# Second attention of a hybrid block: weight sums pinned in program order, the second group's weights loaded ahead of v's copies, the first group's squares in the probabilities' buffers

## The chip, the core and the metric

The kernel runs on one core of one Trainium2 chip, everything in 32-bit floats. The metric is the device time of one launch in microseconds (us); the kernel before was run three times, with a median of 1585.06 us (1583.94 to 1586.10). One more execution was profiled. Its own time was 1586.24 us, of which the profile covers a span of 1584.5 us.

The engines are TensorE (PE, matmuls, with its weight load PEld beside it), VectorE (DVE), ScalarE (ACT), GpSimd (POOL) and SyncE (SP, which issues most DMAs). Each works through its own list of instructions in order and waits where an operand isn't there yet.

## The reference, cut to what matters

The block takes x of 1024 tokens by 512 channels and applies four residual stages: a causal attention with 32 heads of 16 channels, a feed-forward layer with low-rank experts, a second attention, and the feed-forward layer again. The change lies in the second attention:

```python
q = (x @ Wq.T).reshape(b, s, 32, 128).transpose(0, 2, 1, 3)
k = (x @ Wk.T).reshape(b, s, 8, 128).transpose(0, 2, 1, 3)      # v likewise
q, k = _rmsnorm(q, q_norm_w), _rmsnorm(k, k_norm_w)
scores = einsum('bkgqd,bksd->bkgqs', q by groups of 4, k) / sqrt(128)
bias = where(rel > 0, NEG_INF, slope * rel)                      # ALiBi, causal
attn = softmax(scores + bias)
out = einsum('bkgqs,bksd->bkgqd', attn, v);  x = x + out @ Wo.T
```

Here x is layer-normalised before it goes in. There are 8 groups; each has one head of k and v and 4 heads of q.

## The kernel before, in words

**Stages.** The first attention and its feed-forward layer run to about 449 us of the trace, the second attention from there to about 1505 us, the last feed-forward layer to the end. The second attention works group by group (g = 0 to 7), head by head (hh = 0 to 3), and in a head by row tiles of 128 queries (i), from 7 down to 0. A tile's name carries these numbers: p0_1_4 is the scores and then probabilities of group 0, head 1, row tile 4.

**One row tile** (`softmax`, L1044). PE makes the scores of as many keys as the causal mask leaves, in parts of at most 512 keys (L1053). DVE multiplies each part by the query's norm and adds the bias (L1055), takes the row's maximum (L1059) and scales it (L1060); ACT makes the exponentials and their sum (L1062), DVE the reciprocal (L1064), POOL scales the row (L1065). Two row tiles later (`LAG = 2`) `finish` hands it to `columns`, where DVE transposes it in blocks into the tiles pT and tT (L1080, L1086), which leaves p's buffer free. p has four buffers. After a head's last tile PE makes the product with v (`product`, L1114: 128 or more matmuls, 5.6 us), and after the fourth head what is left of all four (`product_rest`).

**Projections by seven products.** Keys and values of a group (`project_kv`, L905), and the queries of two heads at a time (`project_q`, L969; r = 0 or 1), are made by a scheme like Strassen's (`seven`, L865): weights and tokens are each cut into 2 by 2 blocks, and seven products of sums of blocks replace eight products of blocks. Product m takes `left[m]` of the weights and `right[m]` of the tokens, and accumulates in one of two PSUM banks; order `EARLY` is 1, 2, 6, 7, 5, 4, 3 and `STEADY` 1, 6, 2, 7, 5, 4, 3.

- The tokens' sums are made once, a row of 128 columns at a time, by `token_forms` (L848): r5 and r6 on DVE (L851, L852), r7 on POOL (L853), r4 on DVE (L854). Two of the four calls come before the first products, two after the first ones.
- The weights' sums are made in place for each projection by `weight_forms` (L856), both on POOL: a21 += a22 (L861) and then s2 = a21 - a11 into a tile of its own (L862; s_kv or s_q below). Products 5 and 6 read these. Two more sums follow inside `seven`, on POOL too: `left[7]` (L878) after product 1 and `left[3]` (L881) after product 2.
- Keys and queries are normalised late: ACT squares the keys, POOL takes a power for rk (`rsqrt`, L121) and scales the keys (L940), PE transposes them. For queries, ACT squares a head's queries into one work tile that has a single buffer (`square`, L1006; the list `squares` holds heads that wait for it), PE sums the squares with a matmul by ones into a tile of pool `ps_m`, DVE transposes the sums, and POOL takes the power that gives rq (`sum_ready`, `sum_squares`).

**v's copies.** `copies` (L896) spreads each half of v over partitions into va with 16 DMAs on SyncE's queue (L903). The products read va.

**Loads.** `load_qkv` (L796) issues on the same queue the group's wkv (one DMA for k, one for v, L799) and wq (one DMA). wkv and wq have one buffer each, so a group's weights can land only when the projections of the group before are done with them. It is called for group g + 1 at the head of group g.

**How it is interleaved.** Within group g, the work for group g + 1 is cut into small units that a generator `fill` gives out: the keys' and values' projection, `boundary` (one call of `sum_ready`), the out-projection of group g - 1 (`project_o`, L760, not in group 0; it ends in a DMA by POOL that adds into xd, L773), and the two query projections. After each row tile's scores, `fill` is advanced to a number `due`: the group's units (42 in group 0, 74 in the others) times the share of the row tiles done (`SHARE`), capped by `before`, which holds the last 14 units back until after the 26th row tile. In group 0 a second cap of 14 units holds until the 10th.

Entry to the second attention: group 0's weights are loaded early. The code calls `token_forms` for two columns, makes the generators `kv` and `q`, and advances them in turn for 14 units, so that the keys' and the first queries' projections run side by side; then the second query projection follows, and two calls of `sum_ready`.

**What sets the order on an engine.** An instruction that is marked by `tc.keep_in_program_order` is placed where the program's text puts it. All others are placed by a list scheduler, which at build time picks for each engine among the instructions whose operands it models as ready, the earliest in the program first, and those under `tc.high_priority` ahead of them. Before the change the weights' sums are not marked, and the scheduler puts them into gaps of POOL's list.

Of the kernel before, what the change touches and what calls it, by code (L numbers as in the profile page):

```python
# [9 lines left out]
F32 = mybir.dt.float32  # L10
# [54 lines left out]
class Block:  # L65
# [677 lines left out]
    def attention_b(self, ctx, wo_pool, WqT, WkT, WvT, WoT, qw, kw, xnT, xd, missing, ffn_weights):  # L743
# [44 lines left out]
        with ExitStack() as ctx:  # L788
# [4 lines left out]
            ps_m = ctx.enter_context(tc.tile_pool(name="b_m", bufs=2, space=PSUM))  # L793
            ps_o = ctx.enter_context(tc.tile_pool(name="b_o", bufs=1, space=PSUM))

            def load_qkv(g, pinned=False):  # L796
                wkv = wp.tile([P, KC, 2, DB], F32, tag="wkv", name=f"wkv{g}")
                for n, src in enumerate((WkT, WvT)):
                    dma = nc.sync.dma_start(  # L799
                        wkv[:, :, n, :], src[:, g * DB : (g + 1) * DB].rearrange("(k p) n -> p k n", p=P)  # L800
                    )
                    if pinned:
                        tc.keep_in_program_order(dma)
                wq = wp.tile([P, KC, GRP * DB], F32, tag="wq", name=f"wq{g}")
# [3 lines left out]
                return wq, wkv  # L808
# [7 lines left out]
            wq, wkv = load_qkv(0, pinned=True)  # L816


            rels = [self.rel, cp.tile([P, T], F32, tag="relr", name="relr")]
# [28 lines left out]
            def token_forms(a):  # L848

                r = {m: t[:, :, a * P : (a + 1) * P] for m, t in right.items()}  # L850
                nc.vector.tensor_sub(r[5], r[5], r[1])  # L851
                nc.vector.tensor_sub(r[6], r[3], r[5])  # L852
                nc.gpsimd.tensor_tensor(r[7], r[6], r[1], ALU.subtract)  # L853
                nc.vector.tensor_sub(r[4], r[2], r[6])  # L854

            def weight_forms(w, name):  # L856

                blocks = [[w[:, h * H : (h + 1) * H, n] for h in range(2)] for n in range(2)]
                (a11, a12), (a21, a22) = blocks
                s2 = work.tile([P, H, DB], F32, tag="s2", name=f"s2_{name}")  # L860
                nc.gpsimd.tensor_tensor(a21, a21, a22, ALU.add)  # L861
                nc.gpsimd.tensor_tensor(s2, a21, a11, ALU.subtract)  # L862
                return {1: a11, 2: a12, 3: a12, 4: a22, 5: a21, 6: s2, 7: a11}

# [37 lines left out]
                    for a in range(P // B):  # L902
                        nc.sync.dma_start(to[a * B : (a + 1) * B, :, b, :], v_sb[b * B : (b + 1) * B])  # L903

            def project_kv(g, wkv):  # L905
                vs[g] = []
                kT = kTs[g] = kvp.tile([P, T], F32, tag="kT", name=f"kT{g}")
                halves = [kT[:, h * QC : (h + 1) * QC].rearrange("p (i d) -> p i d", d=DB) for h in range(2)]
# [14 lines left out]
                            yield  # L923

                def done():
                    copies(g, 0, v_sb[0])
                    if g:
                        kept.append((g, 1, v_sb[1]))
                    else:
                        copies(g, 1, v_sb[1])  # L930
                    for half, k_sb in enumerate(halves):
                        ssq = sm.tile([P, 4], F32, tag="ssq", name=f"ssq{g}_{half}")
                        for a in range(4):
                            sq = work.tile([P, DB], F32, tag="ksq", name=f"ksq{g}_{half}_{a}")
# [10 lines left out]
                yield from seven(  # L945
                    lambda m: ps_m.tile([P, 4, DB], F32, tag="m", name=f"kv{g}_{m}"),
                    multiply,
                    weight_forms(wkv, f"kv{g}"),
                    *halves,
                    *v_sb,  # L950
                    order=STEADY if g else EARLY,
# [17 lines left out]
            def project_q(g, wq, r, pool=ps_m, tag="m"):  # L969

                if not r:
                    qTs[g] = []
# [16 lines left out]
                            yield  # L989

                def done():
                    squares.extend((g, 2 * r + n) for n in range(2))
                    square()

                if later and (g or r):
# [1 line left out]
                yield from seven(  # L997
                    lambda m: pool.tile([P, QC], F32, tag=tag, name=f"pq{g}_{r}_{m}"),
                    multiply,
                    weight_forms(wq.rearrange("p k (n d) -> p k n d", d=DB)[:, :, 2 * r : 2 * r + 2], f"q{g}_{r}"),  # L1000
                    *(t[:, h * QC : (h + 1) * QC] for t in pair for h in range(2)),
                    order=STEADY if g or r else EARLY,
                    done=done,
# [10 lines left out]
            def sum_ready(behind=False):  # L1014
# [2 lines left out]
                    sum_squares(*squared.pop(0), behind)  # L1017
                square()

            def sum_squares(g, hh, sq_T, behind):  # L1020

                rq = rqs[g][hh]
                st = ps_m.tile([P, QC], F32, tag="m", name=f"st{g}_{hh}")[:, : NT * B]
                for a, sq in enumerate(sq_T.rearrange("p (i a c) -> a p i c", a=P // B, c=B)):
                    with ExitStack() as ctx:
                        if behind:
# [143 lines left out]

            LAG = 2
            wo = load_o(0)
            for a in range(2):
                token_forms(a)
            kv, q = project_kv(0, wkv), project_q(0, wq, 0, ps_s, "s")
            for n in range(7 * H):
                next(kv)  # L1180
                next(q)
# [3 lines left out]
            for n, _ in enumerate(in_turn(kv, q, project_q(0, wq, 1))):  # L1185
                if n == 3:
                    k_columns(*later.pop(0))
            for _ in range(2):
                sum_ready()
            pending = []  # L1190
            fill = iter(())
            heads = list(range(GRP))
# [32 lines left out]
            for g in range(HKV):  # L1225
# [14 lines left out]
                units = 42 + 32 * (g > 0)  # L1240
# [1 line left out]
                for hh in range(GRP):  # L1242
# [205 lines left out]
```

## Time and profile before

| | us |
|---|---|
| median of three runs | 1585.06 |
| the profiled execution's own time | 1586.24 |
| its span | 1584.5 |
| busy: PE | 1548.3 |
| busy: DVE / ACT / POOL | 1079.5 / 594.7 / 486.3 |
| PE busy from 0 to 373 us (first attention) | 369.0 of 373 |
| 373 to 449 (first feed-forward layer) | 76.0 of 76 |
| 449 to 600 (entry and group 0 of the second attention) | 130.0 of 151 |
| 600 to 1505 (its other groups) | 900.8 of 905 |
| 1505 to 1584.5 (last feed-forward layer) | 72.5 of 79.5 |

The first columns of a profile line give a start and a busy time, then the engine, the source line, the operation, the tile written and the tiles read, with sizes in partitions by elements; what stands in brackets is how long the engine had been idle just before, and what it was waiting for. Idle time of an engine costs only where the end of the program depends on it. The granted clock is the share of TensorE's full rate that the chip allowed; over the whole span it was 0.993, and from 449 to 600 us 0.93.

### The profile page before, as it was taken

Reading aid. Unit: us, or ns where it says so; the run is one execution under the profiler, and the core shown is the slowest. Engines: PE = TensorE matmul, PEld = TensorE weight load, DVE = VectorE, ACT = ScalarE, POOL = GpSimd, SP = SyncE. Lnnn points to the kernel's source line nnn. Section 1 sums busy time; section 2 is a strip of 40 time slices with the busy share of each in tenths; the row PEclk is TensorE's granted clock in tenths of the full one; section 3 lists DMA queues with packets and bytes.
Section 4 is the critical chain, followed back from the end, with each engine's and each line's share of the span. In section 5 each row is a group of like instructions: output and inputs, shape, how many; then the busy total and the mean of one; then the engine's idle time right before and its main releaser. Section 6 shows DMA issues by size and latency. Waiting matters only on the chain.

```text
span 1584.5 us, 32254 instructions
## 1 busy us (share of the span) xinstructions
PE 1548.3 (98%) x12894; PEld 928.6 (59%) x12894; DVE 1079.5 (68%) x2789; ACT 594.7 (38%) x1277; POOL 486.3 (31%) x639
## 2 busy tenths in 40 slices
PE   9999999999988899999999999999999999999999
PEld 5545555555555556656755755755665675556664
DVE  4557778773545786777678667677777866777753
ACT  2216656664212433333333333243333333333330
POOL 3000000002243524433443433343344343333450
PEclk9999999999999989999999999999999999999999
DMA  5000222220123101330330231242133022135001
GB/s 206 1 1 6 20 22 19 17 20 18 45 82 94 41 1 53 62 60 28 81 52 21 69 61 41 54 72 50 42 66 67 28 61 35 40 74 126 10 2 53
DMA packets 80951, 75.34 MB, mean 48 GB/s; under 512 B 14945, under 2 KB 56673, under 8 KB 80801
## 3 DMA queue, kind: packets, MB, share of 16 engines
q1 hardware_dynamic: 70272, 52.56, 14.2%
q0 software_dynamic: 8848, 17.58, 7.7%
q10 hardware_dynamic: 1680, 3.15, 0.5%
q8 instruction: 101, 1.65, 0.4%
q14 instruction: 50, 0.40, 0.1%
HBM read 33.08 MB, written 18.87 MB: 33 GB/s over the span
## 4 chain that ended last, share of the span: by engine, by line
PE 86%; DVE 6%; POOL 4%; issue 1%; SPq 1%; ACT 1%; DMA 1%; DVEq 0%; POOLq 0%; ACTq 0%
PE s L1053 14%; PE pq L980 11%; PE o L1114 11%; PE wo L765 11%; PE sT L407 8%; PE kv L914 5%; PE oT L449 5%; PE or L1114 4%; PE pm_f L714 3%; PE s L358 3%; PE pj_v L218 2%; PE pj_q L218 2%; PE pm_ao L1322 2%; PE pj_k L218 2%; DVE p L1055 1%
## 5 line engine op out<-in xcount | busy, mean ns | idle before, releaser
L1062 ACT ACTIVATE p<-p,nm 128x1024 f32<-128x1024 f32 (+7 forms) x256 | 198.4, 775 | 415.5 <-DVE nm L1060 383.3
L1065 POOL TENSOR_SCALAR p<-p,rs 128x1024 f32<-128x1024 f32 (+7 forms) x256 | 192.0, 750 | 406.3 <-DVE rs L1064 392.4
L1053 PE MATMUL s<-kT,qT 128*128 128x512 f32 (+3 forms) x768 | 300.5, 503 | 16.2 <-DVE p L1055 10.9
L1053 PEld LDWEIGHTS s<-kT,qT 128*128 128x128 f32 x768 | 139.4, 192 | 184.2 <-issue 111.4
L765 PE MATMUL wo<-wo,oT 128*128 128x512 f32 x512 | 237.9, 593 | 0.9 <-ACT spare L781 0.9
L1080 DVE STREAM_TRANSPOSE pT<-p 128x512 f32<-128x512 f32 (+3 forms) x256 | 153.9, 603 | 106.5 <-POOL p L1065 63.7
L1059 DVE TENSOR_REDUCE nm<-p 128x1 f32<-128x1024 f32 (+7 forms) x256 | 188.0, 735 | 2.6
L429 ACT ACTIVATE p<-sT 128x512 f32<-128x512 f32 (+1 forms) x292 | 155.2, 592 | 91.0 <-PE s L358 35.2
L1114 PEld LDWEIGHTS o<-pT,va 32*128 32x128 f32 x4212 | 172.9, 185 | 22.3 <-issue 12.5
L1114 PE MATMUL o<-pT,va 32*128 32x224 f32 (+5 forms) x4212 | 181.3, 324 | 0.5 <-DVE pT L1080 0.5
L358 PE MATMUL s<-kT,qT 32*128 32x512 f32 (+3 forms) x768 | 165.2, 520 | 0.0
L407 PE MATMUL sT<-qT,kT 32*128 32x128 f32 (+3 forms) x1152 | 155.9, 402 | 0.7 <-DMA qT<-negT 0.7
L765 PEld LDWEIGHTS wo<-wo,oT 128*128 128x128 f32 x512 | 94.2, 190 | 90.3 <-issue 78.1
L1055 DVE SCALAR_TENSOR_TENSOR p<-s,rq,relr 128x512 f32<-128x512 f32 x192 | 121.4, 648 | 13.6 <-PE s L1053 11.3
L980 PE MATMUL pq<-xnTb,wq 128*128 128x512 f32 x256 | 123.7, 593 | 0.1
L1055 DVE SCALAR_TENSOR_TENSOR p<-s,rq,rel 128x512 f32<-128x512 f32 (+1 forms) x192 | 103.0, 559 | 16.5 <-PE s L1053 16.4
L407 PEld LDWEIGHTS sT<-qT,kT 32*128 32x128 f32 x1152 | 80.8, 184 | 51.0 <-issue 29.4
L1086 DVE STREAM_TRANSPOSE tT<-p 128x512 f32<-128x512 f32 (+3 forms) x128 | 63.9, 499 | 58.1 <-POOL p L1065 30.5
L375 DVE TENSOR_REDUCE part<-s 128x1 f32<-128x512 f32 x128 | 81.6, 685 | 28.1 <-PE s L358 20.1
L508 POOL TENSOR_TENSOR o<-o,over 64x512 f32<-64x512 f32 x12 | 15.2, 1270 | 270.9 <-DMA o<-oTs 113.6
L1064 DVE RECIPROCAL rs<-ss 128x1 f32<-128x1 f32 x256 | 39.9, 156 | 73.6 <-ACT p L1062 73.1
L449 PE MATMUL oT<-p,v_p 128*32 128x128 f32 (+1 forms) x1552 | 88.8, 331 | 0.8 <-DVE turned L472 0.8
(188 smaller groups left out, 2103.9 us busy)
## 6 DMA issues: line engine op xcount, KB each, us to landing
va<-v SPq DMA_DIRECT2D x256, 64.0 KB
xd<-beside POOLq DMA_DIRECT2D x56, 256.0 KB, 4.1
wq<-in_b_WqT_dram SPq DMA_DIRECT2D x8, 1024.0 KB
wo<-in_b_WoT_dram SPq DMA_DIRECT2D x8, 1024.0 KB
x_x<-in_x_dram SPq DMA_DIRECT2D x8, 256.0 KB
wkv<-in_b_WkT_dram SPq DMA_DIRECT2D x8, 256.0 KB
xd<-x_x ACTq DMA_DIRECT2D x8, 256.0 KB
wkv<-in_b_WvT_dram SPq DMA_DIRECT2D x8, 256.0 KB
```

Of the source, the lines that this page charges most:

```text
L358: nc.tensor.matmul(made[j][:, at:end], lhsT=qT[rows_of(j), c, i * P : (i + 1) * P], rhs=kT[rows_of(j), c, kc * QC : kc * QC + end - at], s ...
L407: nc.tensor.matmul(made[j][:, at:end], lhsT=kT[rows_of(j), c, b * P : (b + 1) * P], rhs=qT[rows_of(j), c, qc * QC + x0 : qc * QC + x1], st ...
L429: nc.scalar.activation(p[:, j, :end], made[j][:, :end], AF.Exp)
L449: nc.tensor.matmul(o[rows_of(j), x0 + p0 - at : x0 + p1 - at], lhsT=v_cols(b, c * HC + j), rhs=p[:, j, p0:p1], start=first, stop=last,)
L765: nc.tensor.matmul(ps, lhsT=oTs[g, h][:, t * P : (t + 1) * P], rhs=wo[:, h, :], start=(h == heads[0]), stop=(h == heads[-1]))
L980: nc.tensor.matmul(ps, lhsT=w[:, kc, :], rhs=x[:, kc, :], start=first and kc == 0, stop=kc == H - 1, skip_group_check=True,)
L1053: nc.tensor.matmul(s, lhsT=qT[:, i * P : (i + 1) * P], rhs=kT[:, lo:hi], start=True, stop=True)
L1055: nc.vector.scalar_tensor_tensor(p[:, lo:hi], s, rq[:, i : i + 1], rels[i % 2][:, at + lo : at + hi], ALU.mult, ALU.add)
L1059: nc.vector.tensor_reduce(nm, p[:, :w], AX.X, ALU.max, negate=True)
L1062: nc.scalar.activation(p[:, :w], p[:, :w], AF.Exp, bias=nm, scale=slope, accum_out=ss)
L1065: nc.gpsimd.tensor_scalar(p[:, :w], p[:, :w], rs, 1.0, ALU.mult, ALU.mult)
L1114: nc.tensor.matmul(cols(o[:, a], j, j + skip), lhsT=vs[g][j // 4][rows, j % 4 * NB + b, :], rhs=moving(j, j + skip, rows, slice(b * B, (b ...
```

## The change

All of it lies in the second attention.

- `weight_forms` marks its first sum (a21 += a22) to stay in program order, except for the keys and values and both query projections of group 0. The second sum is not marked. POOL therefore meets the marked sum at the place where the generator that makes it is first advanced (for keys and values, at the head of the group before), behind everything that the program's text puts ahead of it on POOL and that is marked or ready.
- `load_qkv` is split. Group 1's wkv is loaded in `project_kv`'s `done` for group 0, so its two DMAs are issued before v's copies of group 0. The other groups' loads stay where they were.
- At the entry, the weights' sums for the keys and values and for the first queries of group 0 come before the tokens' sums in the program's text; r7 of `token_forms` moves from POOL to DVE.
- Group 0's squares go into four buffers of p's pool as soon as a query projection is done, and the sums of squares into the tile of `ps_o`, the products' PSUM pool. The sums are asked for after units 6 and 9 of the second query projection, and the rest right after the first row tile's scores. The other groups keep the single work tile.
- Group 0's `due` loses both caps, and the order of its fill becomes: keys and values of group 1, first queries, `boundary`, second queries.

```diff
-            def load_qkv(g, pinned=False):
+            def load_kv(g, pinned=False):
...
+            def load_q(g, pinned=False):
...
-                nc.gpsimd.tensor_tensor(r[7], r[6], r[1], ALU.subtract)
+                nc.vector.tensor_sub(r[7], r[6], r[1])
...
-            def weight_forms(w, name):
+            def weight_forms(w, name, pinned=True):
...
-                nc.gpsimd.tensor_tensor(a21, a21, a22, ALU.add)
+                first = nc.gpsimd.tensor_tensor(a21, a21, a22, ALU.add)
+                if pinned:
+                    tc.keep_in_program_order(first)
                 nc.gpsimd.tensor_tensor(s2, a21, a11, ALU.subtract)
...
                 def done():
+                    if not g:
+                        loaded.append(load_kv(1))
                     copies(g, 0, v_sb[0])
...
-                    weight_forms(wkv, f"kv{g}"),
+                    forms,
...
+            def q_forms(g, wq, r):
+                return weight_forms(wq.rearrange("p k (n d) -> p k n d", d=DB)[:, :, 2 * r : 2 * r + 2], f"q{g}_{r}", g > 0)
...
                 def done():
+                    if not g:
+                        for hh in (2 * r + 1, 2 * r):
+                            sq = pp.tile([P, T], F32, tag="p", name=f"qsq{g}_{hh}")
+                            nc.scalar.activation(sq, qTs[g][hh], AF.Square)
+                            squared.append((g, hh, sq))
+                        return
                     squares.extend((g, 2 * r + n) for n in range(2))
                     square()
...
-                st = ps_m.tile([P, QC], F32, tag="m", name=f"st{g}_{hh}")[:, : NT * B]
+                if g:
+                    st = ps_m.tile([P, QC], F32, tag="m", name=f"st{g}_{hh}")[:, : NT * B]
+                else:
+                    st = ps_o.tile([P, NB, QC], F32, tag="o", name=f"st{g}_{hh}")[:, 0, : NT * B]
...
+            kv = project_kv(0, weight_forms(wkv, "kv0", False))
+            q = project_q(0, wq, 0, ps_s, "s", q_forms(0, wq, 0))
             for a in range(2):
                 token_forms(a)
-            kv, q = project_kv(0, wkv), project_q(0, wq, 0, ps_s, "s")
...
-            for _ in range(2):
-                sum_ready()
+                if n in (6, 9):
+                    sum_ready()
+            wkv = loaded[0]
...
-                    wq, wkv = load_qkv(g + 1)
-                    parts.append(project_kv(g + 1, wkv))
-                parts.append(boundary())
+                    if g:
+                        wkv = load_kv(g + 1)
+                    wq = load_q(g + 1)
+                    forms = weight_forms(wkv, f"kv{g + 1}")
+                    parts.append(project_kv(g + 1, forms))
                 if g:
-                    parts.append(project_o(g - 1, wo, heads, ps_m, "m"))
-                if not last:
-                    parts.extend(project_q(g + 1, wq, r) for r in range(2))
+                    parts.extend((boundary(), project_o(g - 1, wo, heads, ps_m, "m")))
+                    parts.extend(() if last else (project_q(g + 1, wq, r) for r in range(2)))
+                else:
+                    parts.extend((project_q(1, wq, 0), boundary(), project_q(1, wq, 1)))
...
+                        while not g and squared and squared[0][0] == 0:
+                            sum_ready()
...
-                            before = 7 * H if not g and n <= NT + LAG else units - 7 * H if n <= 3 * NT + LAG else units
-                            due = min(due, before)
-                            if n in (3 * NT + LAG, 0 if g else NT + LAG):
-                                due = before
+                            if g and n <= 3 * NT + LAG:
+                                due = min(due, units - 7 * H)
+                                if n == 3 * NT + LAG:
+                                    due = units - 7 * H
```

More of the change, by code (lines that the diff above doesn't have):

```diff
@@ L803, in load_qkv @@
                         tc.keep_in_program_order(dma)
+                return wkv
+            def load_q(g, pinned=False):
                 wq = wp.tile([P, KC, GRP * DB], F32, tag="wq", name=f"wq{g}")
@@ L807, in load_qkv @@
                     tc.keep_in_program_order(dma)
-                return wq, wkv
+                return wq
             def load_o(g):
@@ L813, in load_o @@
                 return wo
-            wq, wkv = load_qkv(0, pinned=True)
+            wkv, wq = load_kv(0, pinned=True), load_q(0, pinned=True)
             rels = [self.rel, cp.tile([P, T], F32, tag="relr", name="relr")]
@@ L903, in copies, with project_kv @@
                         nc.sync.dma_start(to[a * B : (a + 1) * B, :, b, :], v_sb[b * B : (b + 1) * B])
-            def project_kv(g, wkv):
+            def project_kv(g, forms):
                 vs[g] = []
@@ L967, in k_columns, with project_q @@
                 nc.scalar.activation(k_sb, ps, AF.Copy, scale=kqw)
-            def project_q(g, wq, r, pool=ps_m, tag="m"):
+            def q_forms(g, wq, r):
+                return weight_forms(wq.rearrange("p k (n d) -> p k n d", d=DB)[:, :, 2 * r : 2 * r + 2], f"q{g}_{r}", g > 0)
+            def project_q(g, wq, r, pool=ps_m, tag="m", forms=None):
                 if not r:
@@ L999, in project_q @@
                     multiply,
-                    weight_forms(wq.rearrange("p k (n d) -> p k n d", d=DB)[:, :, 2 * r : 2 * r + 2], f"q{g}_{r}"),
+                    forms or q_forms(g, wq, r),
                     *(t[:, h * QC : (h + 1) * QC] for t in pair for h in range(2)),
@@ L1018, in sum_ready @@
                 square()
+            loaded = []
             def sum_squares(g, hh, sq_T, behind):
                 rq = rqs[g][hh]
-                st = ps_m.tile([P, QC], F32, tag="m", name=f"st{g}_{hh}")[:, : NT * B]
+                if g:
+                    st = ps_m.tile([P, QC], F32, tag="m", name=f"st{g}_{hh}")[:, : NT * B]
+                else:
+                    st = ps_o.tile([P, NB, QC], F32, tag="o", name=f"st{g}_{hh}")[:, 0, : NT * B]
                 for a, sq in enumerate(sq_T.rearrange("p (i a c) -> a p i c", a=P // B, c=B)):
```

## The prediction

> **What bounds the kernel now.** I read the page's busy times first, then TensorE (PE) in stretches of time, then the timelines of PE, GpSimd (POOL) and SyncE's queue (SPq) inside the poor stretches. The rows by stretch give the busy time of PE, its weight load, DVE, ACT and POOL, then the granted clock, the DMA share and GB/s. In the timelines the columns are start, duration, engine, line, and in brackets the idle time before and its releaser; one f32 matmul stands as two records ("x4" is two matmuls). Tile names below carry group, head and row tile: p0_1_4.
>
> ```profile
> PE 1548.3 (98%) x12894; PEld 928.6 (59%) x12894; DVE 1079.5 (68%) x2789; ACT 594.7 (38%) x1277; POOL 486.3 (31%) x639
> ...
> 440.00:460.00 20.00, 14.17 (x60) 9.06 (x59) 11.60 (x26) 2.34 (x4) 7.84 (x12) 0.86 0.28 75
> 500.00:520.00 20.00, 15.56 (x102) 11.72 (x95) 17.94 (x41) 8.56 (x22) 13.49 (x19) 1.00 0.32 97
> 540.00:560.00 20.00, 15.32 (x34) 7.16 (x33) 12.00 (x32) 4.71 (x13) 8.91 (x11) 0.83 0.09 23
> 560.00:580.00 20.00, 16.68 (x157) 10.42 (x157) 17.35 (x44) 7.98 (x16) 5.11 (x6) 0.93 0.01 2
> 600.00:900.00 300.00, 298.73 (x2370) 192.40 (x2369) 216.20 (x519) 103.92 (x245) 114.44 (x151) 1.00 0.26 54
> 900.00:1200.00 300.00, 298.94 (x2240) 185.35 (x2239) 216.80 (x527) 110.59 (x259) 121.03 (x158) 1.00 0.28 56
> ```
>
> PE binds. From 440 to 600 us it idles 21.0 us (5.83 in 440-460, 0.67, 4.44 in 500-520, 1.51, 4.68, 3.32, 0.58), and its granted clock sags to 0.83-0.93; from 600 to 1500 it idles 4.1 us in 900. So the second attention's entry and first group can give; the seven groups after it can only lose.
>
> ```profile
> 457.51 2.08 PE L914 MATMUL kv<-s_kv,beside 128*128 128x128 f32 x8 [5.83 <-POOL s_kv L862]
> 511.30 2.05 PE L914 MATMUL kv<-s_kv,beside 128*128 128x128 f32 x16 [1.69 <-POOL s_kv L862]
> 551.58 0.80 PE L1053 MATMUL s<-kT,qT 128*128 128x128 f32 x2 [4.68 <-DVE p L1055]
> 578.55 6.21 PE L1053 MATMUL s<-kT,qT 128*128 128x512 f32 x8 [1.45 <-DVE p L1055]
> ```
>
> The third wait comes from further back. POOL takes its instructions in order and stood at the sum of group 2's weights, whose second load stood on SyncE's queue behind 16 copies of v:
>
> ```profile
> 544.04 0.72 POOL L861 TENSOR_TENSOR wkv<-wkv 128x256 f32<-128x256 f32 x1 [7.25 <-DMA wkv<-in_b_WvT_dram]
> 544.72 3.25 POOL L121 TENSOR_TENSOR rq<-rq,mhalf 128x8 f32<-128x8 f32 x2
> ```
> ```profile
> 529.64 11.20 SPq L903 DMA_DIRECT2D va<-v  x16
> 540.88 0.67 SPq L799 DMA_DIRECT2D wkv<-in_b_WvT_dram  x1
> ```
>
> **The change, part by part.**
>
> Entry. Before, POOL runs rs_b (to 453.10), then waits for DVE with L853, and ends s_kv at 457.47. After, the L853 subtractions are DVE's and the weights' sum follows rs_b at once: 453.10 + 0.72 to 0.90 (L861) + 0.08 + 0.73 (L862) = 454.65 to 454.85; the other operand (L852) ends at 454.47. Gain 2.7. DVE gets four subtractions of 0.39-0.46 (row of L851, same shape); two fall into its 8.47 us of idle before 464.67, two stand ahead of the kT addition at 469.47, whose slack is 0.25: cost 0.2, at most 0.4.
>
> The clock at entry: after the 5.83 us of idle the chain took 4.24 us for 20 records, against 2.4 at the rate of 511.30 (32 in 3.84); 1.85 us lost at a granted 0.65. A gap of 3.0 remains. Its nearest row is 1.86 + 1.45 us of idle with 0.5 of work between, before 578.55: granted 0.50 after it, four records in 3.79 us for 1.72. So I take no gain, and keep 1.9 as the upper end. *TensorE: Matmul & The Clock Gate* in the Trainium skill (Part 1, "What's actually happening") puts the drop after an idle window of about 3.4 us; by it a 3.0 us gap escapes and the sum below would be 1.9 better. The row at 578.55 (3.3 us, and not in one piece) leans the other way.
>
> Loads, squares, sums of squares. L861 at 509.71 followed p's scaling with no wait for a DMA, so loading wkv1 earlier buys nothing by itself. On SPq its two issues (0.53, 0.55) now stand after four of va's 32 copies; the other 28 move by 1.1 us, ending near 503, and are first read at 530. Four squares (1.04-1.06 each) take p's four buffers; ACT has 15.61 us of idle before 484.27 for the first, and the sums that free them (0.57 each on PE) stand ahead of p0_0_5. Their PSUM tile is ps_o's only one, each waiting for the DVE transposition before it (0.37), with matmuls between. All nothing; without that cover 0.57 each.
>
> First scores. rq0_0 is ready before the last query addition, so the first p starts at 499.2 instead of 500.40 and its second half at 500.1 instead of 501.06. From there DVE paces: 17.94 of 20 us busy. Adding up its new order by the rows (p 0.66, maximum 1.10 down to 0.2, pT 0.65, v addition 0.6) I reach the last transposition before product o0_0 at 527.9; before it ended at 530.40. Gain 2.5; the wait of 1.69 goes, but DVE's pace takes its place.
>
> The stall at 546.9. The two powers L121 (3.25) and the wait for WvT leave this place: wkv2's sum now stands behind p0_3_0. Late next: rk1_1 (1.03) and four kT scalings (1.41) ahead of p0_1_5, and wq1's sum, now pinned behind p0_1_4, so that s_q1_0 is done near 543.0 where PE asks at 541.3: 1.7 us. Product o0_1 then starts near 551 instead of 562.07. Of these 11.1 us, 1.7 are work that moved behind it (a query unit and half of s0_2_5, 0.86 each), so 9.4 are gained, the 2.5 among them.
>
> From o0_1 to group 1. Idle of 3.89 and 2.07 of slow clock could go; new are s_q1_1 behind rq1_0's power (1.65 + 0.72 + 0.73 after the sum, PE asks 2.0 us too early) and 1.3 of waits for DVE. Gain 2.7. First group together: 12.1. Ends: 6 (only 4.68 plus 2.24 of slow clock, less the new waits; after that stall the query records took 1.71 and the scores 3.11, granted 0.60, 4.82 for what is 0.86 + 1.72 at full rate) and 18.8 (all 14.5 of idle from 500 on and 4.3 of clock).
>
> Group boundary. wkv2's sum and s_kv follow p0_3_0 (done 612.75): 614.2, where kv2_6 ran at 613.96. Cost 0.3, once. In later groups p_3_0 ends at 871.68, s_kv at 873.2, needed at 874.02: hidden by 0.75.
>
> Groups 1 to 6, the price. Before, POOL made these sums long ahead (L861 for q at 744.51, its s_q at 745.88, used at 830.91; s_kv at 836.04, used at 874.02). After, they stand in POOL's order behind a p and a DMA issue; in group 3's times:
>
> ```profile
> 829.02 0.89 POOL L773 DMA_DIRECT2D xd<-beside  x1 [1.03 <-ACT beside L772]
> 830.43 0.79 POOL L1065 TENSOR_SCALAR p<-p,rs 128x640 f32<-128x640 f32 x1 [0.52 <-DVE rs L1064]
> 857.48 0.90 POOL L1065 TENSOR_SCALAR p<-p,rs 128x768 f32<-128x768 f32 x1 [1.03 <-DVE rs L1064]
> ```
> ```profile
> 830.91 1.88 PE L980 MATMUL pq<-beside,s_q 128*128 128x512 f32 x4
> 853.76 1.88 PE L980 MATMUL pq<-xnTb,wq 128*128 128x512 f32 x4
> ```
>
> First pair: the issue ends at 829.91, sum and s_q take 1.5, ready 831.5; PE asks at 830.91: 0.65. Second pair: p_3_5 ends at 858.38, s_q is ready at 859.9; PE, with s_3_4, two units and s_3_3 now put ahead (853.76 + 1.72 + 1.08 + 1.72 + 0.86), asks at 859.13: 0.8. Behind these sums POOL delays p_2_4 and p_3_4 by about 1 us, which the two tiles of lag before a product cover; uncovered it is 0.4 more at the next addition. So 1.45 in each of six groups, 8.7; ends 0 and 11.4.
>
> Sum: 2.7 - 0.2 + 12.1 - 0.3 - 8.7 = 5.6 us faster. The profiled execution took 1586.24 (span 1584.5 and 1.7 around it); 1580.6. The median shown is 1.2 lower: 1579.5.
>
> **Rivals.**
> 1. Slower: the pinned sums stall PE for longer in groups 1 to 6. For it: every us there counts, PE being 99.6% busy. Against: the readiness above is read from events tied to PE's own matmuls. The front gain is 14.3; from 2.4 us per group nothing is left, from 2.9 it is slower by 0.2%; at 3.5 it is 21.0 - 14.3, 1591.8.
> 2. The sums are hidden after all (PE asks later than I read, or the wait only replaces other slack). For it: only 0.65 and 0.8 separate the times. Against: nothing else makes PE wait there. 1585.06 - 14.3 = 1570.8.
> 3. DVE becomes the first group's bound and it gives 6 only. For it: 17.94 and 17.35 of 20 us busy. Against: 12.00 in 540-560, where the stall is. 2.5 + 6 - 0.3 - 8.7 = -0.5: 1585.6, no change.
>
> **How the numbers follow.** Forecast 0.52, rival 1 0.15, rival 2 0.16, rival 3 0.17. A change of 0.2% (3.2 us) is about what a measurement here can tell. Faster: 0.49 of the forecast, rival 2, and 0.02 of rival 3: 0.67. Same: 0.03 and 0.12 from forecast and rival 3: 0.15. Slower: 0.18. The range reaches down to rival 2 and up past rival 3 into the mild part of rival 1: 1570 to 1588; the forecast's own is 1575 to 1583, from its ends in the first group.
>
> **What would show it.** Right: PE's idle in 440-460 down to about 3 us; no wait for WvT on POOL; product o0_1 some 14 us earlier on the clock of the trace; twelve new PE waits of 0.6-0.9 us on s_q from group 1 on, and none on s_kv there. Wrong: such waits of 2 us, waits on s_kv in every group, or a first group in which DVE is busy throughout and PE still idles 10 us.

## The result, and the profile after

The changed kernel takes 1589.70 us (median of 8 runs, 1588.55 to 1590.15), the kernel before 1585.10 (8 runs): a ratio of 1.0029, interval 1.0018 to 1.0040. It is 4.6 us slower, where 5.6 us faster was forecast, and just outside the range (1570 to 1588). The profiled execution took 1589.54, span 1587.8.

The page's busy times and the rows by stretch of the changed kernel, columns as in the prediction:

```profile
PE 1552.9 (98%) x12894; PEld 925.7 (58%) x12894; DVE 1082.1 (68%) x2793; ACT 595.2 (37%) x1277; POOL 484.0 (30%) x635
...
440.00:460.00 20.00, 16.61 (x69) 11.34 (x68) 12.70 (x26) 2.34 (x4) 7.39 (x11) 0.83 0.29 77
500.00:520.00 20.00, 19.50 (x125) 15.53 (x126) 18.79 (x52) 9.28 (x26) 10.37 (x12) 1.00 0.21 64
520.00:540.00 20.00, 16.38 (x160) 10.57 (x159) 14.97 (x34) 7.95 (x20) 8.91 (x16) 0.94 0.31 80
560.00:580.00 20.00, 17.76 (x87) 8.63 (x89) 16.82 (x45) 8.76 (x18) 8.14 (x11) 0.91 0.00 0
600.00:900.00 300.00, 295.43 (x2366) 189.64 (x2367) 211.55 (x507) 104.91 (x249) 113.67 (x148) 1.00 0.25 52
900.00:1200.00 300.00, 296.37 (x2202) 180.77 (x2201) 212.83 (x513) 106.57 (x245) 117.53 (x155) 1.00 0.28 55
```

The two 300-us stretches idle 4.57 and 3.63 us, where they idled 1.27 and 1.06 before. The poor stretches near the entry are fuller, yet 520-540 and 560-580 are poor now. PE's waits in the changed kernel (releaser, total, times, longest) say what is new:

```profile
PE s L1074 <- DVE p L1076: 7.5, 11, 2.2
PE pq L990 <- POOL s_q L867: 6.6, 12, 0.7
PE kv L919 <- DVE beside L855: 3.4, 1, 3.4
...
PE pq L990 <- DVE rs L1085: 1.1, 6, 0.2
```

Twelve waits on s_q, two in each of six groups, were not there before. The start of each product in PE's timeline divides the loss. The whole trace of the changed kernel is 1.55 us ahead already when the second attention begins (448.19 against 449.74), before any code that the change touches; over all the traces here that start lies between 447.63 and 449.74. So times are counted from that first record of the keys' products:

| from the first record of kv, us | before | changed | changed - before |
|---|---|---|---|
| last entry step (first transposition of keys) | 34.41 | 33.14 | -1.27 |
| product o0_0 | 80.80 | 76.87 | -3.93 |
| product o0_1 | 112.33 | 101.31 | -11.02 |
| first `product_rest` (end of group 0's part) | 175.80 | 166.02 | -9.78 |
| the same, one group later | 305.83 | 298.50 | -7.33 |
| last product | 1061.97 | 1066.82 | +4.85 |

The front gains 9.8 us, and each of six groups then gives back 2.44 (132.48 us from one `product_rest` to the next, 130.03 before): 14.6. The difference, +4.85, agrees with the medians' 4.6. Not all that moves is gain or loss: up to product o0_1 the changed kernel has done 1.7 us less work (by its PE records) than the one before, and does it behind.

### The profile page after: what moved, and what is told of

The parts are those of the page before. It is cut to its first block, busy times and chain, and to the rows that moved or that the text cites. A ratio compares the mean times of both kernels' runs of the same rounds, so it can differ in the third digit from the quotient of the medians.

```text
span 1587.8 us, 32286 instructions
## 1 busy us (share of the span) xinstructions
PE 1552.9 (98%) x12894; PEld 925.7 (58%) x12894; DVE 1082.1 (68%) x2793; ACT 595.2 (37%) x1277; POOL 484.0 (30%) x635
## 3 DMA queue, kind: packets, MB, share of 16 engines
q1 hardware_dynamic: 70272, 52.56, 14.3%
## 4 chain that ended last, share of the span: by engine, by line
PE 79%; DVE 9%; POOL 7%; issue 2%; ACT 2%; DMA 1%; SPq 0%; DVEq 0%; POOLq 0%; ACTq 0%
PE s L1074 11%; PE o L1135 10%; PE wo L765 10%; PE pq L990 8%; PE sT L407 8%; PE oT L449 5%; PE kv L919 4%; PE or L1135 4%; PE pm_f L714 3%; PE s L358 3%; DVE p L1076 2%; POOL p L1086 2%; PE pj_v L218 2%; PE pj_q L218 2%; PE pm_ao L1350 2%
## 5 line engine op out<-in xcount | busy, mean ns | idle before, releaser
L1074 PE MATMUL s<-kT,qT 128*128 128x512 f32 (+3 forms) x768 | 297.2, 498 | 10.1 <-DVE p L1076 7.5
L990 PE MATMUL pq<-xnTb,wq 128*128 128x512 f32 x256 | 127.2, 606 | 0.1
```

What stands on the lines that cost most here:

```text
L990: nc.tensor.matmul(ps, lhsT=w[:, kc, :], rhs=x[:, kc, :], start=first and kc == 0, stop=kc == H - 1, skip_group_check=True,)
L1074: nc.tensor.matmul(s, lhsT=qT[:, i * P : (i + 1) * P], rhs=kT[:, lo:hi], start=True, stop=True)
```

## The experiments

All were timed in five rounds beside the kernel before, whose median lay between 1584.4 and 1585.1 in these rounds.

**The late sums unmarked.** The changed kernel, with marks left only on sums that group 0 and the head of group 1 make:

```diff
-                return weight_forms(..., f"q{g}_{r}", g > 0)
+                return weight_forms(..., f"q{g}_{r}", g == 1)
...
-                    forms = weight_forms(wkv, f"kv{g + 1}")
+                    forms = weight_forms(wkv, f"kv{g + 1}", g < 2)
```

> The changed kernel, with the weights' first sums unmarked from group 1 on (queries' sums of groups 2 to 7, keys' and values' sums of groups 3 to 7); everything made in group 0 stays marked. Theory: in the changed kernel's trace a steady group lasts 132.48 us instead of 130.03, six times 2.44 = 14.6, and all of it comes from where POOL meets the queries' sums. So 1589.7 - 14.6 = 1575.1, the group back at 130.0, no PE wait on s_q there. Rival (the longer group comes from something else in the change, such as r7 on DVE or the order of loads): 1588 to 1590, group still 132.5.

Measured: 1574.20 us, ratio 0.9931 (0.9918 to 0.9943); a group is back at 130.04 (613.75 to 743.79 for the first one), and no PE wait on s_q is left in these groups. The whole loss of the steady groups, and more than the whole slowdown, comes from these marks.

**Is it the mark or the place?** Two runs keep the marks, and move the text of the queries' sums. First to the head of the group, which is where the scheduler puts unmarked ones:

```diff
+            def q_sums(wq):
+                for r in range(2):
+                    w = wq.rearrange("p k (n d) -> p k n d", d=DB)[:, :, 2 * r : 2 * r + 2]
+                    a21, a22 = w[:, :H, 1], w[:, H:, 1]
+                    tc.keep_in_program_order(nc.gpsimd.tensor_tensor(a21, a21, a22, ALU.add))
...
                     for at, i in enumerate(...):
+                        if g and not last and not hh and not at:
+                            q_sums(wq)
                         p = softmax(g, hh, i)
```

> The changed kernel; from group 1 on both queries' first sums are marked to stay in program order, but the text makes them at the head of the group, ahead of its first row tile. TensorE's, VectorE's and SyncE's orders are those of the run with late sums unmarked (1574.2), and POOL's differs by one place of the keys' sums. Theory (the mark costs nothing, the place does): 1574.2 within 1, group 130.0 to 130.1. Rival (a mark costs wherever it stands, for instance by waiting for wq's load with p behind it): 1578 to 1590.

Measured: 1574.22 us (ratio 0.9931, 0.9917 to 0.9944), the same as unmarked; a group lasts 130.03. The marks on the keys' and values' sums stand in this run too, where they stood. So in these groups the marks cost nothing by themselves; the late place of the queries' sums does.

Then after the group's sixth row tile (`if g and not last and n == 6`, behind `softmax`):

> The changed kernel; from group 1 on both queries' first sums are still marked to stay in program order, but the text makes them after the sixth row tile of the group instead of when the query projection is first advanced. TensorE's instruction order is that of the run with unmarked sums. Theory (the place costs, not the mark): 1575.1 as there, within 1.5. Rival (marking as such costs, since POOL can no longer be given the sum in a gap): 1583 to 1590. Third: POOL meets the sum while group g+1's wq is not yet landed, PE loses some 1 to 3 us per group: 1581 to 1593.

Measured: 1593.96 us (ratio 1.0057, 1.0044 to 1.0070), slower than all others but one. The third case came nearest, and not for its reason: no instruction of POOL waits for wq's load. In the timelines of POOL, DVE and PE of this run (group 3):

```profile
901.92 1.41 POOL L985 TENSOR_TENSOR wq<-wq 128x256 f32<-128x256 f32 x2
903.30 1.40 POOL L868 TENSOR_TENSOR s_q<-wq 128x256 f32<-128x256 f32 x2
904.67 1.01 POOL L121 TENSOR_TENSOR rk<-rk,mhalf 128x4 f32<-128x4 f32 x1
905.77 1.41 POOL L948 TENSOR_SCALAR kT<-kT,rk 128x128 f32<-128x128 f32 x4
907.16 0.48 POOL L1094 TENSOR_SCALAR p<-p,rs 128x256 f32<-128x256 f32 x1
```
```profile
907.67 0.45 DVE L1109 STREAM_TRANSPOSE pT<-p 128x256 f32<-128x256 f32 x1 [4.50 <-POOL p L1094]
```
```profile
908.80 1.77 PE L1082 MATMUL s<-kT,qT 128*128 128x512 f32 x4 [2.71 <-DVE p L1084]
```

The sums and s_q, 2.8 us, join a power and four scalings of keys ahead of one row tile's p (907.16). DVE waits 4.50 us to transpose that p, its next multiplication of scores (from 908.04) stands behind, and PE waits 2.71 for that. A group lasts 2.6 us longer than unmarked, and 4.1 in the two groups where the granted clock fell behind this wait. So an early place is not a good place: what counts is what stands behind the sum on POOL and when that is wanted.

**One sum of the two.** The kernel with no marks (below), with only the first of the two queries' sums marked:

```diff
-                return weight_forms(..., f"q{g}_{r}", False)
+                return weight_forms(..., f"q{g}_{r}", g > 1 and not r)
```

> The run with no sum marked (1570.7), with the first of the two queries' sums marked again from group 1 on, at the changed kernel's place; TensorE's order stays. In the changed kernel's trace the stretch from the second to the third product of a group, where the first sum stands, is 0.92 longer than before, the next, with the second sum, 1.52. Theory (the two add): 1570.7 + 6 x 0.92 = 1576.2, group 130.95. Rival (the wait is one, and the second only repeats what the first would cost alone): 6 x 2.44, 1585; or hidden in part: 1571 to 1574.

Measured: 1580.06 us (0.9970, 0.9958 to 0.9981), +9.4, a group of 131.62. It is between: the first sum alone costs 1.59 a group, not 0.92, all of it between the second and third product (32.40 us, before 30.80). The wait on s_q is the same 0.46, but in this build the second pair's s_q stands behind the first pair's, ahead of p_2_4 (two s_q from 816.74). DVE waits 1.88 us for that p, ACT's next exponentials wait for DVE, a copy of ACT stands behind them (from 824.02), and PE waits for that copy. In the timelines of POOL, DVE, ACT and PE of this run:

```profile
815.61 1.05 POOL L864 TENSOR_TENSOR wq<-wq 128x256 f32<-128x256 f32 x1
816.74 1.41 POOL L867 TENSOR_TENSOR s_q<-wq 128x256 f32<-128x256 f32 x2
818.13 0.79 POOL L1086 TENSOR_SCALAR p<-p,rs 128x640 f32<-128x640 f32 x1
```
```profile
818.96 0.71 DVE L1101 STREAM_TRANSPOSE pT<-p 128x512 f32<-128x512 f32 x1 [1.88 <-POOL p L1086]
...
823.41 0.61 ACT L1083 ACTIVATE p<-p,nm 128x384 f32<-128x384 f32 x1 [4.95 <-DVE nm L1081]
```
```profile
817.52 1.98 PE L990 MATMUL pq<-beside,s_q 128*128 128x512 f32 x4 [0.46 <-POOL s_q L867]
...
824.64 1.12 PE L990 MATMUL pq<-xnTb,wq 128*128 128x512 f32 x2 [0.30 <-ACT qT L885]
```

The simple addition of two prices falls: moving one sum moved others with it.

**The marks alone.** The kernel before, plus `tc.keep_in_program_order` on every weights' first sum but group 0's own.

> The kernel before, with the one edit that the weights' first sums are marked to stay in program order (all but group 0's own). Theory: six groups lose 2.44 each, 14.6, and group 0 gains what the mark gives there, the sum of group 2's weights no longer ahead of p0_1_5 on POOL: 4.7 of idle and 2.2 of slow clock, less about 2 for the late queries' sums. 1585.1 + 14.6 - 5 = 1594.7 (1592 to 1600). Rival (group 0's gain needs the loads or the squares): 1599 to 1602.

Measured: 1595.29 us (1.0064, 1.0052 to 1.0077), as expected. A group lasts 132.48, and group 0's part ends 171.24 after the first kv record instead of 175.80: the marks alone gain 4.6 there. The 4.68 us wait of before is a 1.75 us wait on s_q in this run.

**No marks at all.** The changed kernel with `False` for every mark.

> The changed kernel with no weights' sum marked at all. Theory: the steady groups are back at 130.0 (-14.6), but in group 0 POOL meets group 2's weights' sum early again and waits for its load behind v's copies: 4.7 of idle and 2.2 of slow clock return, 1589.7 - 14.6 + 6.9 = 1582.0. Rival (the load ahead and the new order of group 0 made that wait go, not the mark): 1575, as with group 0's marks kept.

Measured: 1570.68 us (0.9911, 0.9897 to 0.9925), 14.2 us faster than the kernel before in the same rounds, and below both cases. The wait for the load did not come back: SyncE issues group 2's loads ahead of group 1's copies in this build, and POOL meets the sum with its load done. SyncE's queue, then POOL, of this run:

```profile
522.02 0.51 SPq L799 DMA_DIRECT2D wkv<-in_b_WvT_dram  x1
523.27 10.79 SPq L908 DMA_DIRECT2D va<-v  x16
```
```profile
525.87 0.73 POOL L864 TENSOR_TENSOR wkv<-wkv 128x256 f32<-128x256 f32 x1 [0.34 <-issue]
```

And group 0's marks, which this run lacks and the first one keeps, cost 3.5 us (1574.20 against 1570.68) instead of gaining.

**The parts of the front.** Four runs undo one part each in the kernel with no marks (1570.68). The squares in one work tile again (the `if not g` part of `done` left out):

> The run with no sum marked (1570.7), with group 0's squares back in the single work tile; the early places of the sums of squares stay. The prediction put the four buffers at nothing: 1570.7 within 1. Rival (squares one after another hold up the first rq and so the first scores): 1572 to 1574.

Measured: 1569.72 (0.9904, 0.9890 to 0.9917): no difference that these runs can tell. The load ahead undone (`load_kv(1)` at the head of group 0):

> The run with no sum marked (1570.7), with group 1's keys' and values' weights loaded at the head of group 0 again, behind all 32 copies of v. The prediction held that loading them ahead buys nothing by itself: 1570.7 within 1. Rival: in this build group 2's loads stand behind 16 copies of v again, and POOL meets that sum just ahead of p0_1_4 and waits for the load as before the change, 4.7 of idle and 2.2 of slow clock: 1575 to 1578.

Measured: 1575.47 (0.9939, 0.9926 to 0.9951), +4.8: the rival's number, but mostly not by its cause. In POOL's timeline and SyncE's queue of this run, the wait of before is there again, with its 16 copies:

```profile
507.21 0.73 POOL L864 TENSOR_TENSOR wkv<-wkv 128x256 f32<-128x256 f32 x1
...
542.93 0.72 POOL L864 TENSOR_TENSOR wkv<-wkv 128x256 f32<-128x256 f32 x1 [7.28 <-DMA wkv<-in_b_WvT_dram]
```
```profile
527.57 10.98 SPq L908 DMA_DIRECT2D va<-v  x16
...
539.23 0.55 SPq L799 DMA_DIRECT2D wkv<-in_b_WvT_dram  x1
```

Yet PE has lost most of it earlier. From the first transposition of keys to product o0_0 this run takes 47.95 us, the kernel with no marks 43.73; from there to product o0_1, where the wait for the load stands, 28.36 against 27.39. In PE's timeline of this run, then of the kernel with no marks, group 1's keys' products come some 6 us later and wait for s_kv, whose sum now stands behind two p on POOL (507.21 above):

```profile
504.54 1.95 PE L919 MATMUL kv<-wkv,xnTb 128*128 128x128 f32 x16
508.80 2.46 PE L919 MATMUL kv<-s_kv,beside 128*128 128x128 f32 x16 [2.31 <-POOL s_kv L867]
```
```profile
497.79 1.16 PE L919 MATMUL kv<-wkv,xnTb 128*128 128x128 f32 x8
...
503.23 1.95 PE L919 MATMUL kv<-s_kv,beside 128*128 128x128 f32 x16
```

So 4.2 of these 5.2 us belong to the moved load's own reader, and 1.0 to the load of group 2.

Group 0's caps and old order of fill put back:

```diff
-                    parts.extend((project_q(1, wq, 0), boundary(), project_q(1, wq, 1)))
+                    parts.extend((boundary(), project_q(1, wq, 0), project_q(1, wq, 1)))
...
+                            before = 7 * H if not g and n <= NT + LAG else units - 7 * H if n <= 3 * NT + LAG else units
+                            due = min(due, before)
+                            if n in (3 * NT + LAG, 0 if g else NT + LAG):
+                                due = before
...
```

> The run with no sum marked (1570.7), with group 0's two caps on the units and the old order of its fill (boundary ahead of the queries) put back. The prediction gave these no price of their own. Theory: spreading the units evenly is what feeds TensorE from o0_1 on, where the run with no marks has 548 to 565 us without a wait: 1573 to 1577. Rival (the order hardly matters): 1570 to 1572.

Measured: 1574.09 (0.9929, 0.9916 to 0.9943), +3.4, as the theory had it: its trace has waits of 2.12, 1.45 and 1.26 us between 562 and 574, where the kernel with no marks has one of 1.32. The entry undone:

```diff
-                nc.vector.tensor_sub(r[7], r[6], r[1])
+                nc.gpsimd.tensor_tensor(r[7], r[6], r[1], ALU.subtract)
...
-            kv = project_kv(0, weight_forms(wkv, "kv0", False))
-            q = project_q(0, wq, 0, ps_s, "s", q_forms(0, wq, 0))
             for a in range(2):
                 token_forms(a)
+            kv = project_kv(0, weight_forms(wkv, "kv0", False))
+            q = project_q(0, wq, 0, ps_s, "s", q_forms(0, wq, 0))
```

> The run with no sum marked (1570.7), with the entry undone: r7 on POOL again, the tokens' sums ahead of the weights' in the text. The prediction put the entry at 2.7 - 0.2 = 2.5: 1573.2. The changed kernel's trace says 1.3 (5.83 of idle became 3.39, but 0.3 more of slow records and 0.3 + 0.5 of later waits took some back): 1572.0 (1571.5 to 1572.5).

Measured: 1571.68 (0.9916, 0.9903 to 0.9930), +1.0, as expected; but the runs of the kernel with no marks themselves lie between 1569.55 and 1572.14, so this difference is uncertain by about its own size.

**A version better than both.** In the kernel with no marks the largest wait left in group 0 is 2.34 us at 535.95, behind one p for which POOL is late: it first makes two powers and eight scalings of keys. For group 1's keys the scalings go to ACT:

```diff
+                            if g == 1:
+                                nc.scalar.activation(k_sb[:, a, :], k_sb[:, a, :], AF.Copy, scale=rk[:, a : a + 1])
+                            else:
                                 nc.gpsimd.tensor_scalar(...)
```

> The run with no sum marked (1570.7), with group 1's keys scaled by ACT instead of POOL. In that run POOL does two powers and eight scalings of keys (4.9 us) ahead of p0_1_5, DVE waits 4.1 us for that p and PE 2.3 for DVE at 535.95, and PE's clock sags to 0.91 behind. TensorE's order stays. Theory: 2.8 of POOL's 4.9 go, most of PE's 2.3 and of some 1.5 of slow clock with it: 1567.5 (1566.5 to 1569). Rival (the two powers alone hold p, or ACT's own order takes the place): 1570 to 1572.

Measured: 1567.06 us (0.9886, 0.9873 to 0.9900), as expected: 17.4 us faster than before and the fastest of all. The wait is 0.41 now, and the clock is whole. PE's timeline and the row of the stretch, of this run:

```profile
534.32 1.13 PE L1077 MATMUL s<-kT,qT 128*128 128x512 f32 x2 [0.41 <-DVE p L1079]
```
```profile
520.00:540.00 20.00, 18.06 (x165) 11.20 (x164) 16.67 (x39) 10.84 (x31) 7.63 (x10) 1.00 0.31 81
```

## Why the prediction was wrong, point by point

**The steady groups: mechanism and place right, the term too small (8.7 forecast, 14.6 measured).** The prediction priced two waits on s_q, 0.65 and 0.8 a group (the first a little high by its own figures: 829.91 + 1.5 is 831.4, so 0.5). In PE's timeline of group 3 (changed kernel) the idle is 0.46 and 0.65; taken from start to start against before, PE loses 0.61 and 0.81 at these places:

```profile
820.32 1.88 PE L990 MATMUL pq<-xnTb,wq 128*128 128x512 f32 x4
822.65 1.98 PE L990 MATMUL pq<-beside,s_q 128*128 128x512 f32 x4 [0.46 <-POOL s_q L867]
...
851.98 1.98 PE L990 MATMUL pq<-beside,s_q 128*128 128x512 f32 x4 [0.65 <-POOL s_q L867]
853.80 1.02 PE L990 MATMUL pq<-xnTb,wq 128*128 128x512 f32 x2
854.66 0.81 PE L1074 MATMUL s<-kT,qT 128*128 128x384 f32 x2
855.66 1.96 PE L990 MATMUL pq<-beside,wq 128*128 128x512 f32 x4 [0.19 <-DVE rs L1085]
```

That is 1.42 of the 1.45 forecast. The other 1.02 us of the 2.44 was left out. The first four records after each wait take 1.83 and 1.82 where they took 1.71 and 1.72, at a granted clock of 1.00: 0.2. The records of scores at 830.07 lose 0.2, and no run shows why. And from 855.3 on, 0.36 and then 0.26 go to an addition of DVE that comes late, with what follows it. This chain stands in the timelines of POOL and DVE (changed kernel, group 3; 128x640 is p_3_4), then in DVE's of before, where DVE had no wait at that place:

```profile
850.39 0.73 POOL L864 TENSOR_TENSOR wq<-wq 128x256 f32<-128x256 f32 x1
...
853.40 0.80 POOL L1086 TENSOR_SCALAR p<-p,rs 128x640 f32<-128x640 f32 x1
```
```profile
854.23 0.71 DVE L1101 STREAM_TRANSPOSE pT<-p 128x512 f32<-128x512 f32 x1 [1.04 <-POOL p L1086]
854.86 0.65 DVE L889 TENSOR_TENSOR qT<-qT,pq 128x512 f32<-128x512 f32 x1
```
```profile
862.80 0.71 DVE L1080 STREAM_TRANSPOSE pT<-p 128x512 f32<-128x512 f32 x1
```

The addition ends at 855.51, PE goes on at 855.66. The step that failed is the sentence that the two tiles of lag cover POOL's later p_2_4 and p_3_4: the prediction itself put the uncovered price at 0.4 at the next addition, and set it to nothing. For p_3_4 it was 0.62. The other 0.4 us, slower records without a wait, had no term at all. The run with the sums after the sixth row tile shows the same chain (POOL, a p, DVE, PE) at 2.6 to 4.1 us a group.

Most of the signs that the prediction gave for being right came true: 3.4 us of idle at the entry, no wait for WvT on POOL, product o0_1 12.6 us earlier on the clock of the trace, twelve waits on s_q of 0.46 and 0.65, and one small wait on s_kv. They could not tell a group that loses 1.45 us from one that loses 2.44, since they counted only the waits on s_q.

**The entry: 2.5 forecast, 1.3 in this trace, 1.0 by the run that undoes it, 2.1 on the mean of all thirteen traces.** The idle fell from 5.83 to 3.39, near the forecast 3.0. What released PE was not s_kv but L855, which the prediction had ready at 454.47, by its row at full speed. With r7 on DVE and all the sums on POOL at once, DVE's subtractions took twice their time (below). The second wait, behind one more subtraction of DVE, is 0.94 instead of 0.60. The clock took its share after 3.39 us of idle, as the prediction assumed, but not always the same share: by the trace's records of the granted clock it was half for 6.8 us here, and for 3.4 us in seven of the nine other traces with the same entry. Those ten traces have the first transposition of keys at 31.90 to 33.38 us, mean 32.6; the three with the old entry at 34.41 to 35.05, mean 34.7.

**Up to product o0_1: 11.1 forecast, 9.75 measured (from the entry's end), with the wrong cause.** The wait for group 2's load did go from POOL's list. The prediction laid it to the mark alone, and said that loading wkv1 earlier buys nothing by itself. Both are enough: the marks alone removed the wait in the kernel before, and the load ahead alone removes it in the kernel with no marks, because the built order then has group 2's loads ahead of group 1's copies. Undoing the load brings back 4.8, and by the trace most of it at its own reader: the prediction saw no wait for that load's DMA in the trace before, and did not ask where the scheduler would put the sum and the keys' products once the load was early. So the 2.5 forecast up to product o0_0 came (2.65 from the entry's end) but for another reason than the one given: without the load ahead the stretch is 47.95 us, no better than before (46.39), and without the four square buffers 44.31. No run undoes the early sums of squares alone. The wait of 1.7 us on s_q1_0 that was forecast is there with the marks alone (1.75), but not in the changed kernel: PE has then waited 2.13 us behind a p (536.23), for which POOL is late by two powers and eight scalings of keys, the clock has fallen behind that wait, and s_q is ready when PE comes.

**From o0_1 to the end of group 0's part: 0.7 gained forecast (2.7, less 1.7 of moved work and 0.3 at the boundary), 1.24 lost.** The waits of 1.86 and 1.45 went, and a wait of 2.24 at 566.71 took their place, with 1.8 us of slow records behind it (four records of the query products take 3.52 us from 568.34 on, 1.72 at full rate); PE's whole idle there is 3.54 us, before 3.90. The two runs with and without group 0's marks differ by 3.5 us, and of these two the wait at 566.71 is there only with them. The 2.0 us on s_q1_1 that the prediction counted there did not show: PE, late by then, takes s_q at 571.86, ready at 571.81. What it did not count is the order of PE's products that the marks bring: with them 2.6 us more of work stand behind o0_1. That this order makes the wait of 2.24 is a reading of the traces; no run changes the order alone.

**The squares** at nothing were right (-1.0, inside the spread of the runs). The boundary's 0.3 is in the trace (0.32 on s_kv at 602.07).

The sum: the front was 14.3 forecast and 9.8 measured, the groups 8.7 and 14.6. So two things failed: the groups' term, by what the lag was said to cover, and the front's, by 4.5 (1.2 at the entry, 1.4 up to o0_1, 1.9 behind it). Rival 1 named the right danger and a fair threshold, 2.4 us a group, which is what a group lost. With the front as it was, 1.63 a group was enough (9.8 / 6).

## What to carry to other kernels

A small sum on an engine with a third of its time busy is free only where nothing that is wanted soon stands behind it in that engine's order. Before a mark fixes a place, look at what it displaces: here the same two marked sums cost 0, 2.4 or 2.6 to 4.1 us a group by their place alone. When an instruction's wait is priced, price the chain behind it too, or measure one period of the loop from start to start, which holds everything. And if a load moves, ask what the scheduler will do with its readers, and read the whole queue again: here the moved load's own reader gained about 4 us where nothing had waited for the DMA, and the next group's load another 1.

## What the runs showed of the hardware

**The clock often falls after shorter idle than forecast.** The prediction's rows had half clock after 5.83 us of idle, after 4.68, and after 1.86 + 1.45. In the changed kernel 2.13 and 2.24 us were enough. The rows by stretch around those two waits (536.23 and 566.71), then two rows of the run with the sums after the sixth row tile, behind two of its waits of 2.71 us (ending at 774.6 and 908.8):

```profile
536.00:538.00 2.00, 1.77 (x4) 1.01 (x5) 1.97 (x6) 0.03 (x1) 0.00 (x0) 0.86 0.04 9
538.00:540.00 2.00, 2.00 (x4) 0.75 (x3) 1.67 (x4) 0.89 (x2) 0.82 (x2) 0.50 0.00 0
540.00:542.00 2.00, 2.00 (x6) 1.15 (x5) 2.00 (x9) 1.25 (x4) 1.84 (x3) 0.78 0.00 0
...
568.00:570.00 2.00, 2.00 (x6) 0.95 (x5) 2.00 (x9) 2.00 (x4) 1.89 (x2) 0.54 0.00 0
```
```profile
774.00:778.00 4.00, 3.36 (x5) 1.71 (x6) 3.48 (x8) 1.09 (x2) 0.65 (x2) 0.57 0.86 196
...
908.00:914.00 6.00, 5.20 (x42) 3.20 (x46) 5.51 (x12) 1.83 (x3) 2.20 (x4) 1.00 0.61 143
```

By the trace's records of the granted clock it is half for 3.4 us each time, beginning 1.2 and 1.5 us after the restart; after the 1.32 us wait of the kernel with no marks it stays 1.00. It is not a fixed rule of idle time: over all the traces here, 14 of 15 waits of PE between 2.1 and 2.4 us in group 0 were followed by half clock, but only two of the six waits of 2.71 us in the run with the sums after the sixth row tile, and no single wait below 1.8 us. Where it falls, half clock for 3.4 us costs up to 1.7 us more: with the keys' scalings moved, the stretch between the first two products is 2.7 us shorter, 1.6 of it idle and the rest records that are no longer slow. The idle window of about 3.4 us that *TensorE: Matmul & The Clock Gate* in the Trainium skill states (Part 1, "What's actually happening") did not hold as a lower bound in these runs.

**VectorE at half speed beside GpSimd.** From 451.5 to 456.9 POOL streams without a pause in the changed kernel, and DVE's subtractions of one shape take 0.85 to 0.95 there, 0.39 before and 0.41 behind it. The last row is of the kernel before: there the same two subtractions (L852, now L855) take 0.38 each, while POOL stands idle until 454.27:

```profile
450.41 0.39 DVE L854 TENSOR_TENSOR xnTb<-xnTb 128x256 f32<-128x256 f32 x1
452.56 1.69 DVE L855 TENSOR_TENSOR beside<-xnTb 128x256 f32<-128x256 f32 x2
454.17 0.94 DVE L856 TENSOR_TENSOR beside<-beside,xnTb 128x256 f32<-128x256 f32 x1
...
456.78 0.41 DVE L857 TENSOR_TENSOR beside<-xnTb,beside 128x256 f32<-128x256 f32 x1
```
```profile
453.71 0.76 DVE L852 TENSOR_TENSOR beside<-xnTb 128x256 f32<-128x256 f32 x2
```

*SBUF — State Buffer* in the Trainium skill ("SBUF: two separate sides") says that a VectorE operation with two SBUF inputs and a GpSimd operation that reads SBUF take turns on one shared pair of ports. These rows fit that; they show that the time doubles while POOL streams, not by what mechanism. While both engines were busy here, a subtraction moved from POOL to DVE took DVE twice the time it takes alone.
